# Gated recurrence times a two-layer windowed-attention block: layernorm transposes on half the array's rows, PSUM as one tile of seven banks, and the task order as a table

## The chip, the core and the metric

One NeuronCore of a Trainium2 chip runs the kernel. The metric is the device time in microseconds; the time before is the median of three runs. One more execution was recorded by the hardware profiler, and the profile, its views and its trace all come from that one.

The engines are named as in the profile: PE is the TensorE matmul unit (PEld its weight loads), DVE is VectorE, ACT is ScalarE, POOL is GpSimd, SP is SyncE, which issues the DMAs. PSUM is the memory that PE writes and that DVE and ACT read and write. The kernel uses eight banks of it: seven for its work, each 128 partitions by 512 numbers, and one for a small tile `norms`.

## What is computed

The input `x` is 16 sequences of 512 tokens with 128 channels, in float32. The reference, cut to what matters:

```python
xn = layernorm(x)
# the recurrence
xc = causal_depthwise_conv(xn, conv_w, conv_b)          # 4 taps
r, i = sigmoid(xc @ W_r.T + b_r), sigmoid(xc @ W_i.T + b_i)
a = sigmoid(log_a) ** (8 * r)
h[t] = a[t] * h[t-1] + sqrt(clip(1 - a*a, 0))[t] * (i * xc)[t]
s = rmsnorm(h @ W_out.T) * gamma
# two layers of attention and feed-forward, on xn
for l in range(2):
    hs = shift_token(y)                                  # half the channels one token late
    q, k, v = split(hs @ wqkv)                           # 8 heads of 64
    q, k = rotary_xpos(l2norm(q) * qs, l2norm(k) * ks)
    o = softmax(mask(8 * q @ k.T)) @ v                   # windows of 64 tokens, this and the one before
    y = y + o @ wo
    f = layernorm(shift_token(y)) * lg + lb
    a, g = split(f @ w1 + b1)                            # 341 each
    y = y + (a * gelu(g)) @ w2 + b2
out = x + s * silu(y)
```

## The kernel before

**Tiles.** A sequence (index `s`, 0 to 15) is four token tiles of 128. The recurrence and the feed-forward work on a whole sequence at a time, with channels on the partitions and 512 tokens along the free axis. Attention works on one token tile (`n`, 64 per layer), with tokens on the partitions for the products `q`, `k`, `v`, and on pairs of tiles (`m`, 32 per layer) for the output projection.

**Tasks.** The work is written down as about 6,500 tasks in `all_work`. A task has a name, an item, an engine and the tiles that it opens or touches. The names that the text uses:

- `ld` loads a sequence; `fbn`, `fag`, `fpw`, `fnm` are its layernorm; `ftx` transposes it to channel-major on PE, `xp` and `xs0` copy that out of PSUM on ACT.
- `c0` to `c3` and `cv` are the convolution, `gr`, `gi` the gates' matmuls, `sc` the scan, `yo` the output matmul of the recurrence.
- `Q`, `K`, `V` are the projections on PE. `sqq`, `sqk` square them on ACT, `rq1`, `rq2`, `rk1`, `rk2` are the rotary products on DVE, `addq`, `addk` and `nrm` finish them on POOL, with `red` and ten small steps `n0` to `n9` on DVE for the norms.
- `tr` transposes q and k on PE, into two banks, one for each half of the array's rows; four copies `kc0`, `kc1`, `qc0`, `qc1` on ACT bring them to SBUF. `sim` is the scores on PE (with the mask as a matmul of its own), into two banks.
- `nmA`, `nmB` are the maxima on DVE, `exA`, `exB` the exponentials with their sums on ACT, `rA`, `rB` the reciprocals on DVE, `PA`, `PB` the scaling on POOL. `PT` transposes the weights on PE, into two banks, `pT0` and `pT1` copy them out on ACT, `PV` is the product with the values, `oT` its copy, `wo` the output projection, `y` its addition on DVE.
- Per layer `l` and sequence: `ltx`, `lbn`, `lag`, `lpw`, `lnm`, `lth`, `lhT` are the layernorm, with two transposes on PE (`ltx` to token-major, `lth` back) and the affine copy `lhT`; `lg`, `la`, `lge`, `lhi`, `lyy`, `lr0`, `lr1` are the feed-forward.
- `tf`, `tn`, `z`, `zs`, `zx`, `ot` are the last transpose, the silu, and the output.

**Order.** `schedule` sets the order of the tasks, and with it each engine's own order. It keeps a clock for each engine and picks, among the tasks that can start soon, the one with the smallest key (a due time, corrected by the tables `TAU` and `SHIFT`). It also gives each PSUM tile its bank. The program is then recorded task by task in that order, and the recording layer puts in the semaphores.

**PSUM.** Each of the seven work banks is a pool of its own, and each use of a bank is a tile of its own with its own name (`q`, `sA`, `o`, ...):

```python
banks = [ctx.enter_context(tc.tile_pool(name=f"bank{i}_", bufs=1, space=PSUM)) for i in range(BANKS)]
...
at[key] = banks[bank].tile([P, INNER], F32, name=key[1], tag="bank")
```

**Tile forms of PE.** A matmul can use the array whole, by halves of its rows, by halves of its columns, or by quarters. The planner prefers the form that PE is in. The six transposes of the layernorms and of the end (`ftx`, `0tx`, `0th`, `1tx`, `1th`, `tf`) use it whole, `tr` and `PT` by row halves, `sim` by quarters, `PV` and `wo` by column halves. The helper `matmul` (the projections, gates and feed-forward) takes the whole array where PE stands in that form, and two column halves else.

Of the kernel before, what the change touches and what calls it, by code (L numbers as in the profile page):

```python
# [30 lines left out]
REACH = 30  # L31
OTHER_MODE = 300
TABLE_KEY = {"ea": "TA", "exA": "TE", "exB": "TE", "rt": "TR"}

ROOM = {
    "0mv": 4, "1mv": 4, "fmv": 3, "g": 2, "gelu": 3, "h": 1, "hT": 2, "hid": 3, "kT": 4, "lx": 1, "max": 8,
    "ms": 3, "nx": 2, "oT": 2, "pT": 2, "pr": 3, "qT": 2, "rot": 4, "s": 4, "sq": 2, "sw": 4, "th": 3, "thi": 2,
    "thr": 2, "vl": 4, "vs": 5, "x": 1, "xS": 5, "xc": 2, "xn0": 1, "xn1": 1, "xnf": 1, "xp": 2, "xtok": 2, "y": 3,
}

TAU = {
    "0a": 216, "0ag": 580, "0bn": -24, "0g": -260, "0ge": 4076, "0hT": -537, "0hi": 2408, "0nm": -68, "0pw": -1261,
    "0r0": 990, "0r1": -2182, "0th": 276, "0tx": 33, "0yy": 4216, "1a": 5294, "1ag": 711, "1bn": -852, "1g": 2433,
    "1ge": 377, "1hT": 69, "1hi": 1970, "1nm": 2033, "1pw": -138, "1r0": -467, "1r1": 3335, "1th": 1298,
    "1tx": 1736, "1yy": 5460, "K": -201, "PA": -1630, "PB": -211, "PT": -5584, "PV": 5164, "Q": -112, "TA": -870,
    "TE": -1741, "TR": -256, "V": 1007, "a2": 2422, "addk": 342, "addq": 331, "c0": 2390, "c1": 4732, "c2": -600,
    "c3": -880, "cv": 4159, "ea": 4106, "exA": 6642, "exB": 6438, "fag": 293, "fbn": 1372, "fnm": 6908,
    "fpw": -474, "ftx": 1447, "gelu": -193, "gi": -1858, "gr": -1619, "in": 687, "kc0": 96, "kc1": 219, "kz": -623,
    "ld": 317, "m": -1641, "mp": -882, "ms": 196, "n0": -604, "n1": -429, "n2": -114, "n3": -1713, "n4": 216,
    "n5": 4588, "n6": -2054, "n7": 964, "n8": 241, "n9": -1574, "nmA": -1790, "nmB": 892, "nrm": -1410, "oT": 1064,  # L50
    "ot": -20, "pT0": -35, "pT1": 493, "qc0": -51, "qc1": 577, "rA": 3056, "rB": 2230, "red": 2587, "rk1": 2345,
    "rk2": 414, "rq1": 966, "rq2": -382, "rt": 6134, "s2": -85, "sc": 5466, "si": 123, "sim": -1328, "sqk": 4277,
    "sqq": 2127, "sr": 988, "ss": -495, "tf": 241, "tn": 4128, "tr": 28, "u": 305, "vc": 153, "vd": 10, "vz": 229,
    "wo": 2798, "xld": 4155, "xp": 513, "xs0": 4048, "xs1": -411, "y": 221, "yo": -419, "z": 254, "zs": 8223,
    "zx": 79,
}

SHIFT = {
    "x": (-481, -1082, -101, 4130, 4541, -2524, -596, -258, 3490, -259, 2561, 600, 228, 314, -1342, -1808),
    "g": (27, -265, -606, -62, -144, -220, 324, -273, -28, -213, 296, -716, 121, -138, 542, -30),  # L60
    "a0": (350, -20, 342, 124, 73, 33, 45, -145, 120, 6, 33, 121, 23, 100, 23, -747),
    "f0": (-268, -741, -170, -150, -78, -208, -321, -26, -268, 17, 69, 64, -154, -367, -424, 38),
    "a1": (491, 246, 7, 125, 21, 9, 412, -60, 139, 236, 260, 323, 25, -521, 1127, 175),
    "f1": (-27, -141, -79, 167, 315, -53, -198, 120, 203, 307, 537, 1298, 1006, 4076, 961, 4073),
# [3 lines left out]
ENGINES = ("PE", "ACT", "DVE", "POOL", "SP")  # L68
AFTER = (
    (0, 210, 220, 225, 225), (200, 120, 160, 150, 160), (220, 177, 120, 160, 160), (96, 85, 65, 0, 60), (2400,) * 5,  # L70
)
SWITCH = (110, 115, 100, 97)
WHOLE, ROWS, QUARTERS, COLUMNS, EITHER = range(5)
LOCKED = "sc", "m", "addq", "addk", "nrm", "PA", "PB", "a2", "u", "zs", "zx"
ROUND, SIM_ROUND = 0, 0
GATED, AHEAD = True, 9
PAUSE = 1000, 3500
TOGETHER = 1
RELOAD = 1450
EXP, GELU, ROOT = 1, 2, 4  # L80


class Work:

    def __init__(self):
        self.names, self.tasks, self.known, self.tiles, self.keys, self.touch = {}, [], {}, [], [], []
        self.stage = self.seq = None  # L90

    def tile(self, kind, *item):
        k = (kind, *item)
        if k not in self.known:
            self.known[k] = len(self.tiles)
            self.tiles.append(kind)
            self.keys.append(k)
            self.touch.append([])
        return self.known[k]

    def add(self, name, item, engine, span, base, after=(), opens=(), touches=(), mode=EITHER, table=0, late=None):

        i, e = len(self.tasks), ENGINES.index(engine)
        self.names[name, item] = i
        opens = [self.tile(*t) for t in opens]
        touches = [self.tile(*t) for t in touches]
        lock = name in LOCKED
        for t in {*opens, *touches}:
            self.touch[t].append(i)
        self.tasks.append(dict(  # L110
            name=name, item=item, stage=self.stage, seq=self.seq, engine=e, span=span, key=base, after=[self.names[a] for a in after],
            opens=opens, touches=[*opens, *(t for t in touches if t not in opens)], mode=mode, table=table, lock=lock,
            late=late,
        ))


def all_work(B, NT, lag=2, lead=1, vdve=(), early=EARLY):
    w = Work()
    add = w.add

    def ln(p, s, base, src, after):
        add(p + "bn", s, "DVE", 780, base, after, touches=[src], opens=[(p + "mv", s)])
        add(p + "ag", s, "DVE", 285, base, [(p + "bn", s)], touches=[(p + "mv", s)])
        add(p + "pw", s, "POOL", 1940 if p == "f" else 1330, base, [(p + "ag", s)], touches=[(p + "mv", s)])
        add(p + "nm", s, *(("ACT", 1550) if p == "f" else ("DVE", 1280)), base, [(p + "pw", s)], touches=[src, (p + "mv", s), ("xn" + p, s)], opens=[("xn" + p, s)] if p == "f" else [])

    def gates(s):
        b = s - lead
        w.stage, w.seq = "x", s
        add("ld", s, "SP", 60, b, opens=[("xtok", s)], late=3500)  # L130
        ln("f", s, b, ("xtok", s), [("ld", s)])
        add("ftx", s, "PE", 450, b, [("fnm", s)], mode=WHOLE, opens=[("bank", "fx", s), ("xp", s), ("xS", s)], touches=[("xnf", s)])
        add("xp", s, "ACT", 480, b, [("ftx", s)], touches=[("xp", s), ("bank", "fx", s)])
        add("xs0", s, "ACT", 480, b, [("ftx", s)], touches=[("xS", s), ("bank", "fx", s)])
        add("xs1", s, "POOL", 700, b, [("xp", s), ("xs0", s)], touches=[("xp", s), ("xS", s)])
        w.stage = "g"
        on_pe, C = s < early, ("bank", "cv", s)
        if on_pe:
            add("c0", s, "DVE", 720, b, [("xp", s)], opens=[("xc", s)], touches=[("xp", s)])
            add("cv", s, "PE", 1714, b, [("xp", s)], opens=[C], touches=[("xp", s)])  # L140
            add("c1", s, "DVE", 660, b, [("cv", s)], touches=[("xp", s), C])
            add("c3", s, "DVE", 660, b, [("c0", s), ("c1", s)], touches=[C, ("xc", s)])
        else:
            add("c0", s, "DVE", 720, b, [("xp", s)], opens=[C], touches=[("xp", s)])
            for k in (1, 2, 3):
                add(f"c{k}", s, "DVE", 660, b, [(f"c{k-1}", s)], opens=[("xc", s)] if k == 3 else [], touches=[("xp", s), C])
        for g in "ri":
            add("g" + g, s, "PE", 857, b, [("c3", s)], opens=[("bank", g, s)] + [("thr", s)] * (g == "r"), touches=[("xc", s)])
            add("s" + g, s, "ACT", 600, b, [("g" + g, s)], touches=[("bank", g, s)] + [("thr", s)] * (g == "r"), table=EXP | GELU)
        add("ea", s, "ACT", 720, b, [("sr", s)], touches=[("thr", s)], table=EXP)  # L150
        add("in", s, "DVE", 660, b, [("si", s)], opens=[("thi", s)], touches=[("bank", "i", s), ("xc", s)])
        add("a2", s, "POOL", 1250, b, [("ea", s)], touches=[("thr", s)], opens=[("g", s)])
        add("m", s, "DVE", 320, b, [("a2", s)], touches=[("g", s)])
        add("rt", s, "ACT", 628, b, [("m", s)], touches=[("g", s)], table=ROOT)
        add("u", s, "POOL", 1250, b, [("rt", s), ("in", s)], touches=[("g", s), ("thi", s)])
        add("sc", s, "DVE", 1130, b, [("u", s)], touches=[("thr", s), ("thi", s)], opens=[("h", s)])
# [102 lines left out]
    for s in range(B):  # L259
        gates(s)  # L260
    for l in range(2):
# [4 lines left out]
        for s in range(B):  # L266
            forward(l, s)
# [797 lines left out]
```

## Time and profile before

| | us |
|---|---|
| median of three runs | 1335.42 |
| lowest and highest | 1334.04, 1335.59 |
| the profiled execution, its own time | 1334.82 |
| its span, first to last instruction | 1333.0 |
| PE busy | 1281.7 |
| ACT busy | 1156.0 |
| DVE busy | 1098.5 |
| POOL busy | 1039.9 |

The profile's page has the span, each engine's busy time, then the span in 40 slices with a digit for each engine's busy share and one for the clock that TensorE was granted (9 is full). A group of instructions is given by line, engine, operation and tile, then how often, the busy time, the mean of one in ns, and the idle time before them with what ended it. The table of stretches has, for each stretch of the span, the busy time and number of instructions of each engine, and then the granted clock, the share of the DMA engines and GB/s. A row of the waits has who waited for whom, the time in all, how often, and the longest. A row of the timeline has start and length in us, then the engine, line, operation and tiles. The mean clock over the span is 0.992.

### The profile page before, as it was taken

Reading aid. Unit: us, or ns where it says so; the run is one execution under the profiler, and the core shown is the slowest. Engines: PE = TensorE matmul, PEld = TensorE weight load, DVE = VectorE, ACT = ScalarE, POOL = GpSimd, SP = SyncE. Lnnn points to the kernel's source line nnn. Section 1 sums busy time; section 2 is a strip of 40 time slices with the busy share of each in tenths; the row PEclk is TensorE's granted clock in tenths of the full one; section 3 lists DMA queues with packets and bytes.
Section 4 is the critical chain, followed back from the end, with each engine's and each line's share of the span. In section 5 each row is a group of like instructions: output and inputs, shape, how many; then the busy total and the mean of one; then the engine's idle time right before and its main releaser. Section 6 shows DMA issues by size and latency. Waiting matters only on the chain. (4 is left out here: it accounts for less than half of the span.)

```text
span 1333.0 us, 43632 instructions
## 1 busy us (share of the span) xinstructions
PE 1281.7 (96%) x16988; PEld 729.0 (55%) x16988; DVE 1098.5 (82%) x2752; ACT 1156.0 (87%) x3716; POOL 1039.9 (78%) x1009
## 2 busy tenths in 40 slices
PE   6699999999999999999999999999999999999997
PEld 2355455565555656555564565555646655664563
DVE  7978888988989879788887977989798889848854
ACT  5697989899898989989898988989989979996892
POOL 6896789697887969779696995988778787854862
PEclk9899999999999999999999999999999999999999
DMA  6011011111111111102021111110111011110111
GB/s 207 1 46 33 3 32 33 26 42 33 33 42 38 30 25 38 42 22 65 6 54 25 38 34 33 42 30 22 38 25 46 22 25 38 34 46 21 26 46 40
DMA packets 46766, 49.42 MB, mean 37 GB/s; under 512 B 4704, under 2 KB 31456, under 8 KB 46560
## 3 DMA queue, kind: packets, MB, share of 16 engines
q1 hardware_dynamic: 46560, 46.63, 14.1%
q8 instruction: 135, 2.21, 0.7%
q14 instruction: 71, 0.58, 0.1%
HBM read 13.05 MB, written 4.19 MB: 13 GB/s over the span
## 5 line engine op out<-in xcount | busy, mean ns | idle before, releaser
L722 POOL TENSOR_TENSOR rot<-rot,sw 128x512 f32<-128x512 f32 x256 | 326.2, 1284 | 69.2 <-DVE rot L715 42.0
L846 POOL TENSOR_TENSOR pr<-pr,sum 128x512 f32<-128x512 f32 x256 | 265.1, 1049 | 75.9 <-DVE sum L840 61.0
L759 POOL TENSOR_TENSOR rot<-rot,y 128x1024 f32<-128x1024 f32 x128 | 242.8, 1916 | 37.7 <-DVE y L754 37.3
L832 ACT ACTIVATE pr<-sA,max 128x128 f32<-128x128 f32 x512 | 191.3, 461 | 13.6 <-DVE max L825 7.9
L832 ACT ACTIVATE pr<-sB,max 128x128 f32<-128x128 f32 x512 | 191.3, 458 | 0.6 <-DVE y L754 0.6
L727 DVE TENSOR_REDUCE norms<-sq 128x16 f32<-128x1024 f32 x128 | 155.3, 1213 | 4.9 <-ACT sq L708 2.9
L857 ACT COPY pT<-p 128x512 f32<-128x512 f32 x256 | 151.2, 672 | 5.5 <-PE p L854 4.8
L832 ACT ACTIVATION_READ_ACCUMULATOR pr<-sB,max 128x1 f32 x512 | 145.8, 298 | 0.0
L832 ACT ACTIVATION_READ_ACCUMULATOR pr<-sA,max 128x1 f32 x512 | 145.1, 300 | 0.0
L625 PE MATMUL q<-wqkv,xS 128*64 128x512 f32 (+1 forms) x486 | 136.4, 612 | 4.4 <-ACT pr L832 2.5
L866 PEld LDWEIGHTS o<-pT,vl 128*64 128x64 f32 x2048 | 110.5, 137 | 47.9 <-issue 27.4
L785 ACT COPY qT<-t 128x256 f32<-128x256 f32 x256 | 112.3, 450 | 27.0 <-PE t L780 26.6
L625 PE MATMUL k<-wqkv,xS 128*64 128x512 f32 (+1 forms) x482 | 133.7, 601 | 2.0 <-ACT pr L832 1.6
L625 PE MATMUL v<-wqkv,xS 128*64 128x512 f32 (+1 forms) x464 | 133.5, 604 | 0.9 <-ACT pr L832 0.8
L819 PE MATMUL sA<-kT,qT 64*64 64x128 f32 x2048 | 133.6, 269 | 0.0
L819 PE MATMUL sB<-kT,qT 64*64 64x128 f32 x2048 | 133.2, 269 | 0.0
L866 PE MATMUL o<-pT,vl 128*64 128x64 f32 x2048 | 128.3, 224 | 0.3 <-ACT pT L857 0.3
L866 PE MATMUL o<-pT,vs 128*64 128x64 f32 x2048 | 126.4, 222 | 0.5 <-ACT pT L857 0.4
L819 PEld LDWEIGHTS sA<-kT,qT 64*64 64x64 f32 x2048 | 119.9, 133 | 9.0
L884 PE MATMUL x<-oT,wo 128*64 128x257 f32 x1024 | 123.3, 382 | 0.4 <-ACT pr L832 0.2
L819 PEld LDWEIGHTS sB<-kT,qT 64*64 64x64 f32 x2048 | 119.7, 133 | 0.0
L718 DVE TENSOR_TENSOR sw<-q,table 128x512 f32<-128x512 f32 x128 | 87.4, 683 | 33.7 <-PE q L625 31.0
(154 smaller groups left out, 3206.5 us busy)
## 6 DMA issues: line engine op xcount, KB each, us to landing
vl<-vs SPq DMA_DIRECT2D x224, 128.0 KB, 2.2
xtok<-in_x SPq DMA_DIRECT2D x16, 256.0 KB, 3.1
x<-in_x SPq DMA_DIRECT2D x16, 256.0 KB, 3.1
out<-th SPq DMA_DIRECT2D x16, 256.0 KB, 2.4
wqkv<-in_wqkv SPq DMA_DIRECT2D x2, 768.0 KB, 6.7
w<-in_w SPq DMA_DIRECT2D x2, 384.0 KB, 6.3
rot<-in_rope SPq DMA_DIRECT2D x1, 512.0 KB, 5.6
wo<-in_wo SPq DMA_DIRECT2D x2, 256.0 KB, 5.2
```

Of the source, the lines that this page charges most:

```text
L625: nc.tensor.matmul(ps[col : col + step], w[:, col : col + step], v, start=start, stop=stop)
L718: nc.vector.tensor_tensor(two(at["sw", *n, "qk"[i]]), two(src)[:, :, ::-1, :], two(tab), ALU.mult)
L722: nc.gpsimd.tensor_tensor(r, r, at["sw", *n, "qk"[i]], ALU.add)
L727: nc.vector.tensor_reduce(at["nx", *pair(n)][:, 0, 16 * j : 16 * j + 16], sq, AX.X, ALU.add)
L759: nc.gpsimd.tensor_tensor(flat, flat, bc(at["y", *pair(n)][:, 0, 16 * j : 16 * j + 16], DH), ALU.mult)
L785: nc.scalar.copy(at["qT", *n][:, :, 64 * w : 64 * w + 64], four(at["bank", f"t{w}", *n])[:, 0])
L819: nc.tensor.matmul(out_(w, par)[:, p, :], q[r, p, half[w]], k[r, p, col : col + P], start=False, stop=p == 3)
L832: nc.scalar.activation(at["pr", *n][:, g, :], sim[:, p, :], AF.Exp, bias=at["max", *n, h][:, p : p + 1], accum_out=at["sum", *n][:, g : g ...
L846: nc.gpsimd.tensor_tensor(w, w, bc(at["sum", *n][:, g], P), ALU.mult)
L857: nc.scalar.copy(at["pT", *n][:, w], heads(at["bank", f"p{w}", *n]))
L866: nc.tensor.matmul(o[64 * par : 64 * par + 64, p, 64 * w : 64 * w + 64], at[("vl", "vs")[w], *n][:, h * DH : (h + 1) * DH], pT[:, w, 4 * p ...
L884: nc.tensor.matmul(ps[64 * r : 64 * r + 64, 0 : 2 * P + 1], w, o[:, k, 1 - r : 2 * P + 2 - r], start=k == 0, stop=k == 3)
```

## The change

Three things change together.

1. The six kinds of layernorm and final transposes work on half the array's rows at a time: eight transposes of 64 rows in place of four of 128. The two row halves go to two neighbouring banks (a `pair`), and whoever reads them (`xp`, `xs0`, `lbn`, `lnm`, `lhT`, `tn`, `z`) reads both banks with one access pattern; `z` is two instructions in place of one. `matmul` always uses column halves, so that the form of the whole array is gone.
2. `tr`, `sim` and `PT` also write to a pair of neighbouring banks. The copies `kc0`, `kc1` become one `kc`, `qc0`, `qc1` one `qc`, and `pT0`, `pT1` one `pT`, each over both banks. The seven banks are one PSUM tile, and what a task opens is a slice of it.
3. `all_work` and `schedule` are replaced by `all_tasks`, which only lists the tasks and what they open, and by two tables found by a local search: `PLACES` (each task's place in the order, as steps from one of its kind to the next) and `FIRST_BANK` (the bank, or the first of the two). `in_order` sorts by place.

```diff
-TAU = {
...
-SHIFT = {
...
+PLACES = {
+    "ld": "0 1 7 18 62 120 150 21 1038 175 292 486 483 382 186 598",
+    "fbn": "2 2 12 43 135 36 161 25 1069 128 292 485 485 421 141 605",
...
+FIRST_BANK = {
+    "ftx": "0043025350322002",
...
-def all_work(B, NT, lag=2, lead=1, vdve=(), early=EARLY):
...
-def schedule(w, tau, shift, room):
...
+def all_tasks(B, NT):
...
+                add(n, ("tr", [("pair", "t", *n), ("qT", *n)]), "kc", "qc", ("sim", [("pair", "s", *n), ("pr", *n)]))
...
+def in_order(tasks):
+
+    order, of_name = [], {}
+    for t in tasks:
+        of_name.setdefault(t[0], []).append(t)
+    for name, these in of_name.items():
+        places = np.cumsum([int(v) for v in PLACES[name].split()])
+        for k, (place, t) in enumerate(zip(places, these)):
+            b = int(FIRST_BANK[name][k]) if name in FIRST_BANK and tasks[t] else 0
+            order.append((place, t, b))
+    return sorted(order)
...
-    banks = [ctx.enter_context(tc.tile_pool(name=f"bank{i}_", bufs=1, space=PSUM)) for i in range(BANKS)]
...
+    banks = ctx.enter_context(tc.tile_pool(name="banks", bufs=1, space=PSUM)).tile([P, BANKS, INNER], F32, name="banks")
...
         if kind == "bank":
-            at[key] = banks[bank].tile([P, INNER], F32, name=key[1], tag="bank")
+            at[key] = banks[:, bank, :]
+        elif kind == "pair":
+            at[key] = banks[:, bank : bank + 2, :]
...
+    def halves(ps):
+
+        return ps[:, :, 0 : 64 * NT].rearrange("p r (t k) -> p t r k", k=64)
+
+    def by_halves(v):
+        return v.rearrange("p (t r k) -> p t r k", r=2, k=64)
+
     def transposed(ps, src):
+
         for t in range(NT):
-            nc.tensor.transpose(ps[:, t * P : (t + 1) * P], src[:, t, :], c["ident"])
+            for r in range(2):
+                rows = slice(64 * r, 64 * r + 64)
+                nc.tensor.transpose(ps[:, r, 64 * t : 64 * t + 64], src[rows, t, :], c["ident"][rows, rows])
 
     def token_major(ps, src):
+
         for t in range(NT):
-            nc.tensor.transpose(ps[:, t * P : (t + 1) * P], src[:, t * P : (t + 1) * P], c["ident"])
+            for r in range(2):
+                rows = slice(64 * r, 64 * r + 64)
+                nc.tensor.transpose(
+                    ps[:, r, 64 * t : 64 * t + 64], src[rows, t * P : (t + 1) * P], c["ident"][rows, rows]
+                )
 
     def matmul(ps, w, v, start=True, stop=True):
 
-        step = P if tiling == WHOLE else 64
-        for col in range(0, P, step):
-            nc.tensor.matmul(ps[col : col + step], w[:, col : col + step], v, start=start, stop=stop)
+        for col in range(0, P, 64):
+            nc.tensor.matmul(ps[col : col + 64], w[:, col : col + 64], v, start=start, stop=stop)
...
-    def keep_q(n, w):
-        nc.scalar.copy(at["qT", *n][:, :, 64 * w : 64 * w + 64], four(at["bank", f"t{w}", *n])[:, 0])
...
+    def keep_q(n):
+        nc.scalar.copy(windows(at["qT", *n]), four(at["pair", "t", *n])[:, :, 0])
...
-    def keep_weights(n, w):
-        nc.scalar.copy(at["pT", *n][:, w], heads(at["bank", f"p{w}", *n]))
+    def keep_weights(n):
+        nc.scalar.copy(at["pT", *n].rearrange("p w h d -> p w (h d)"), at["pair", "p", *n])
...
-        th, v = at["th", s], tok(at["bank", "tf", s])
+        th, v = at["th", s].rearrange("p t (r k) -> p t r k", k=64), halves(at["pair", "tf", s])
         if i == 0:
             nc.scalar.activation(th, v, AF.Tanh, scale=0.5)
         else:
-            nc.vector.scalar_tensor_tensor(th, th, 1.0, v, ALU.add, ALU.mult)
+            for r in range(2):
+                part = th[:, :, r, :]
+                nc.vector.scalar_tensor_tensor(part, part, 1.0, v[:, :, r, :], ALU.add, ALU.mult)
...
-    for i, mine, tiling in order:
...
+    for _, t, bank in in_order(tasks):
+        for key in tasks[t]:
+            open_tile(key, bank)
+        do[t[0]](t[1])
+        for f in behind.get(t, ()):
             f()
```

## The prediction

> **What bounds the kernel now.** The page first: the span, the busy shares, the clock row.
>
> ```profile
> span 1333.0 us, 43632 instructions
> PE 1281.7 (96%) x16988; PEld 729.0 (55%) x16988; DVE 1098.5 (82%) x2752; ACT 1156.0 (87%) x3716; POOL 1039.9 (78%) x1009
> ...
> PEclk9899999999999999999999999999999999999999
> ```
>
> TensorE is the bound: 96% busy at almost full clock. But three further engines are busy around 80% at the same time. The busy times of PE, DVE and ACT alone add up to 3,536 us inside 1,333. The kernel lives by their overlap. The waits of TensorE come next, the longest first.
>
> ```profile
> PE fx L615 <- ACT xnf L605: 11.9, 1, 11.9
> PE i L625 <- DVE xc L649: 5.4, 1, 5.4
> PE t L780 <- POOL rot L759: 4.4, 8, 1.0
> PE p L854 <- ACT pr L832: 3.4, 1, 3.4
> ```
>
> These are start-up and single events. In steady state nothing holds TensorE. The table of stretches shows what that looks like in the middle, and what the clock does near gaps:
>
> ```profile
> core 0: us, PE busy (x) PEld busy (x) DVE busy (x) ACT busy (x) POOL busy (x), PEclk, DMA share, GB/s
> 400.00:500.00 100.00, 99.91 (x1348) 56.70 (x1348) 85.17 (x207) 89.60 (x300) 77.69 (x74) 1.00 0.13 31
> ...
> 37.90:41.30 3.40, 1.78 (x2) 0.83 (x3) 3.16 (x13) 0.00 (x0) 0.40 (x1) 0.50 0.00 0
> 41.30:44.70 3.40, 3.40 (x5) 0.96 (x3) 3.40 (x18) 1.35 (x2) 2.70 (x2) 0.50 0.00 0
> 44.70:48.10 3.40, 3.40 (x49) 1.71 (x52) 2.31 (x11) 2.44 (x7) 3.40 (x3) 0.99 0.03 7
> 92.50:95.90 3.40, 2.00 (x40) 1.55 (x32) 2.80 (x4) 3.40 (x8) 3.23 (x5) 1.00 0.02 5
> 95.90:99.40 3.50, 3.05 (x12) 1.26 (x8) 2.92 (x7) 3.50 (x16) 1.82 (x4) 0.51 0.25 75
> 130.10:133.50 3.40, 1.87 (x22) 1.06 (x24) 2.69 (x17) 0.36 (x2) 3.06 (x2) 1.00 0.18 42
> 133.50:136.90 3.40, 3.40 (x20) 1.15 (x18) 2.18 (x6) 1.33 (x6) 3.23 (x4) 0.50 0.00 0
> ```
>
> 100 us of the middle hold 275 us of PE, DVE and ACT work together. And a stretch of 3.4 us in which TensorE was busy 55% or 59% is followed by one at half clock; one at 52% under half clock leaves it there; a full one gives the clock back.
>
> Last, the timeline of the start, where one engine has to wait for the other, for the price of a hand-over.
>
> ```profile
> 11.86 1.63 PE L615 MATMUL fx<-squares,xnf 128*128 128x128 f32 x4 [11.86 <-ACT xnf L605]
> 13.52 0.58 ACT L944 COPY xp<-fx 128x512 f32<-128x512 f32 x1 [0.56 <-PE fx L615]
> 14.01 0.58 ACT L633 COPY xS<-fx 64x512 f32<-64x512 f32 x1
> 14.22 0.92 DVE L647 TENSOR_SCALAR xc<-xp,cols 128x512 f32<-128x512 f32 x1 [4.75 <-ACT xp L944]
> ```
>
> PE ends at 13.49, ACT starts at 13.52; ACT ends at 14.10, DVE starts at 14.22. A hand-over costs 0.03 to 0.12 us after the end, and a copy that is followed by another on its engine costs 0.49 instead of 0.58, because only the last of a run pays its full length.
>
> **The change, part by part.**
>
> *What is meant to be saved.* Per layernorm transpose four 128x128 matmuls become eight on half the rows, two at a time. The rows near it:
>
> ```profile
> L780 PE MATMUL t<-squares,rot 64*128 64x64 f32 x2048 | 89.8, 229 | 5.9 <-POOL rot L759 4.4 <-ACT pT L857 1.0 <-ACT pr L832 0.4
> L619 PE MATMUL 0tx<-squares,xS 128*128 128x128 f32 x64 | 11.1, 289 | 1.3 <-DVE xS L891 1.3
> ```
>
> Start to start in the timeline, sixteen half transposes take 0.50 us, so eight take 0.25; four whole ones take 0.44. 96 such tasks (six per sequence) save 96 x 0.19 = 18 us. Switches between TensorE's tile forms fall from 659 to 621 in the built order; at about 0.1 us (the gap between runs of two forms) 4 us. Joining two copies into one saves ScalarE's fixed part: 450 ns for 256 columns and 672 for 512 give 228 fixed, times 384 joined pairs = 87 us, but of an engine that is not the bound: counted as nothing while TensorE covers it. ACT gets 7 more table loads of 1.28 us, DVE 16 more `z` halves: under 15 us, covered too. With all else equal: about -22 us.
>
> *What else moves.* All seven banks become slices of one tile, `banks`. The built programs can be read without running them, and I read what each instruction waits for. Before, an instruction on PSUM is preceded, in program order, by one on another engine 5,925 times, and waits for that preceding run in 820. After, there are 3,497 such hand-overs, and 3,469 of them wait for the last instruction of the run just before, whatever its bank. A stretch from the middle (lines of the changed kernel, waits in semaphore counts):
>
> ```
> ACT L679 sqq  reads bank 5                      -> ACT 1093
> PE  L754 tr   writes banks 0,1  waits ACT 1093  -> PE 5458
> DVE L689 rk2  reads bank 2      waits PE 5458   -> DVE 1389
> ACT L848 oT   reads bank 6      waits DVE 1389  -> ACT 1094
> PE  L596 Q/K/V writes bank 5    waits ACT 1094  -> PE 5460
> ```
>
> The copy of bank 6 waits for a product from bank 2, which waits for transposes into banks 0 and 1. So the tile is ordered as a whole: all PSUM work of PE, ACT and DVE is one chain in the order of the table. Each engine's queue stands behind its waiting instruction; POOL and the DMA queue, which feed on them, go idle rather than late. The cover under which three engines worked at once is gone.
>
> *The price of the chain*, from the rows of before, start to start within a run (PE 0.86 for a projection, DVE 0.60 and ACT 0.48 for 512 columns, ACT 1.38 for four exponentials with their sums):
> - PE: 384 Q, K, V + 288 feed-forward + 32 gates at 0.86 = 605; 128 scores at 1.11 = 142; 256 flips at 0.50 = 128; 128 `o` at 0.93 = 119; 64 `x` at 1.74 = 111; 96 transposes at 0.25 = 24; `yo`, `cv` 19. Sum 1,147.
> - ACT: 256 exponentials 353; 128 `pT` of 1,024 columns at 0.92 (two rows' slope carried on) 118; 256 `qT`, `kT` 123; 256 `sq` 123; `vs`, `oT` 123; gelu 56; the rest 69. Sum 965.
> - DVE: 512 rotations 309; 256 maxima 154; `hid`, residuals, `xS` 128; `xn`, statistics 66; taps, `s`, `thi`, `th` 70. Sum 727.
> - 3,497 hand-overs: what the last of a run takes beyond its step (PE 0.17, ACT 0.19, DVE 0.08), plus 0.03 to 0.12 to the next engine: about 0.20 each, 700.
> - DVE and ACT have 528 us of work off PSUM (`norms` reduction, the ten small steps, reciprocals, scan; `xnf`, table loads). In front of a queue it can delay the chain: between 0 and 528; a third, 175, since an engine idles most of the time until its turn.
> - before the first matmul 11.9, after the last 7.3: 19.
>
> At full clock 1,147 + 965 + 727 + 700 + 175 + 19 = 3,733 us.
>
> *The clock.* Those 1,285 PE runs have a mean of 0.9 us, then 2.0 us of other engines. With what it drains, PE is busy about 1.06 of 2.9 us, 37%: below the 55 to 59% that cost the clock above. At half clock it is 2.0 of 3.8, 52%: at the share that did not give it back. The Trainium skill ("TensorE: Matmul & The Clock Gate", section "What's actually happening") says in my words that the half rate comes after a wholly idle window of about 3.4 us. No gap here is that long as a rule, so by that page the clock stays and the sum is 3,733; by the rows it is lost most of the time. I take the rows: 85% of PE's work at half clock, + 0.85 x 1,147 = 975. Ends: 0 and 1,147.
>
> A second rule speaks against the chain: "PSUM — Partial Sum Buffer", section "PSUM bank collisions raise a hardware error", asks for semaphores by bank, not for more, and says that engines on different banks run clean side by side; stretch 400 to 500 agrees. By it the waits are needless, and the sum would be -22. But waits that stand in the program are kept, needless or not.
>
> Sum: 3,733 + 975 = 4,708 against the profiled execution's span of 1,333.0 (1334.8 with what lies around it, 0.6 below the median of 1335.42). I say 4,700.
>
> **The rivals.**
> 1. *The chain, but full clock*: 3,733, with hand-overs from 0.14 to 0.26 and the uncovered work from 0 to 528 some 3,350 to 4,300. For it: the stretch 1321 to 1325 (62% busy) kept its clock, so the edge is near 60%, and long feed-forward runs may hold it. Against: 37% is far below.
> 2. *Faster: the waits are there but come late enough to be free.* Place: each hand-over. If the table were laid so that the earlier instruction is done whenever its follower's turn comes, only the 22 us remain, and perhaps 5 of the start: about 1,308. It needs each wait to be shorter than its engine's own backlog; but the backlog of TensorE is 96% and its follower on ACT cannot begin before it, so it decides at once, from the first hundred hand-overs on. It would also hold if the waits that I read were not those that run.
> 3. *Half a chain*: runs within one engine grow, hand-overs overlap more than I think: 2,500 to 3,400.
>
> **How the numbers follow.** Chain with lost clock 0.78 (own range 4,050 to 5,400: uncovered work, hand-overs and clock share at their ends), chain at full clock 0.15, half a chain 0.03, faster 0.04. The predicted time is that of the first. The range, 3,700 to 5,300, takes most of the first and the middle of the second. Slower by over 0.2% (about what a measurement of this kernel can tell from no change) 0.955, faster 0.04, the rest 0.005.
>
> **What would show it.** In the page after: PE, DVE, ACT shares that together come near 100% (PE about 50% with half clock, 37% without), PE waits in the hundreds of us behind ACT and DVE on other tiles, all named `banks`; PEclk mostly 5; POOL near 25%. In the chain of waits PE, ACT and DVE in turn, where now a few engines lead. The transposes' group halved in TensorE time at equal clock. Wrong would be: PE over 90% busy (rival 2), PEclk at 9 (rival 1), or ACT and DVE busy at once with PE in most stretches.

## The result, and the profile after

| | us |
|---|---|
| before, median (lowest to highest) | 1335.08 (1334.04 to 1335.59) |
| after, median (lowest to highest) | 4698.7 (4697.5 to 4702.4) |
| ratio, with its 95% interval | 3.520 (3.514 to 3.526) |

The changed kernel takes three and a half times as long. The page of its profile, the same rows as before:

```profile
span 4700.5 us, 45000 instructions
...
PE 2484.1 (53%) x17688; PEld 1088.7 (23%) x17688; DVE 1168.2 (25%) x2768; ACT 1242.0 (26%) x3339; POOL 1040.9 (22%) x1009
...
PEclk6555555555555555555555555565555555555555
```

DVE, ACT and POOL have about the work that they had: 1,168 against 1,099 us, 1,242 against 1,156, 1,041 against 1,040. PE has twice its busy time, at half its clock. What is gone is the overlap: the shares of PE, DVE and ACT add up to 104% of the span, where they were 265%. The table of stretches has it in the middle of the run (columns as before: PE, PEld, DVE, ACT, POOL, then the clock):

```profile
400.00:500.00 100.00, 50.59 (x328) 20.22 (x328) 26.78 (x56) 28.94 (x88) 20.07 (x19) 0.52 0.01 2
2000.00:2100.00 100.00, 52.17 (x352) 20.84 (x344) 25.16 (x53) 27.98 (x77) 24.42 (x20) 0.55 0.03 7
```

Laid over each other, the records of the three engines say the same. Before, all three were busy at once for 935 of 1,333 us. After, they are for 10 of 4,700; for 4,107 us exactly one of them is busy, for 205 none.

The waits, all engines, longest first, and then those of TensorE alone (who waited for whom: us in all, times, longest):

```profile
POOL pr L820 <- DVE sum L814: 1070.8, 118, 63.5
POOL rot L693 <- DVE rot L686: 514.8, 49, 31.2
...
DVE max L799 <- PE banks L596: 227.7, 73, 6.5
```

```profile
PE banks L596 <- ACT pr L806: 198.9, 72, 7.0
PE banks L596 <- DVE max L799: 119.9, 67, 5.1
PE banks L596 <- DVE rot L686: 103.1, 57, 3.8
```

Before, TensorE's longest wait was 11.9 us, once, at the start. Now the matmuls of one helper (L596: projections, gates, feed-forward) wait for exponentials (`pr`), maxima and rotary products, whose results they don't use. The largest sums are POOL's; it is starved, and nothing waits long for it. The timeline shows how one such wait leads to the next. A projection of the kernel before comes first, for its length, then the changed kernel:

```profile
408.81 1.03 PE L625 MATMUL q<-wqkv,xS 128*64 128x512 f32 x4
```

```profile
2012.71 1.01 ACT L831 COPY pT<-banks 128x1024 f32<-128x1024 f32 x1 [4.09 <-PE banks L840]
2013.78 0.29 PEld L596 LDWEIGHTS banks<-wqkv,xS 128*64 128x64 f32 x4 [1.30 <-ACT pT L831]
2013.78 1.98 PE L596 MATMUL banks<-wqkv,xS 128*64 128x512 f32 x4 [1.11 <-ACT pT L831]
2015.87 0.69 DVE L799 TENSOR_REDUCE max<-banks 128x4 f32<-128x512 f32 x1 [4.04 <-PE banks L596]
...
2016.59 0.59 ACT L848 COPY oT<-banks 128x512 f32<-128x512 f32 x1 [2.87 <-DVE max L799]
...
2017.23 1.97 PE L596 MATMUL banks<-hT,w 128*64 128x512 f32 x4 [1.48 <-ACT oT L848]
```

The copy of the weights, a projection, a maximum of some scores, the copy of an attention output, a feed-forward matmul: five steps on different data. By the order table they use banks 0 and 1, then 2, 4, 5 and 0, and each begins 0.03 to 0.11 us after the one before it ends. A projection takes 1.98 us, where it took 1.03 at full clock (0.86 to the next start and 0.17 beyond). The small steps of the norms (DVE L705 to L723) run in between, since they touch only SBUF and the tile `norms`.

### The profile page after: what moved, and what is told of

Same layout as the page of the kernel before. It is cut to its first block, busy times and chain, and to the rows that moved or that the text cites. A ratio compares the mean times of both kernels' runs of the same rounds, so it can differ in the third digit from the quotient of the medians.

```text
span 4700.5 us, 45000 instructions
## 1 busy us (share of the span) xinstructions
PE 2484.1 (53%) x17688; PEld 1088.7 (23%) x17688; DVE 1168.2 (25%) x2768; ACT 1242.0 (26%) x3339; POOL 1040.9 (22%) x1009
## 5 line engine op out<-in xcount | busy, mean ns | idle before, releaser
L596 PE MATMUL banks<-wqkv,xS 128*64 128x512 f32 x1536 | 740.6, 1064 | 613.2 <-ACT pr L806 94.7
L820 POOL TENSOR_TENSOR pr<-pr,sum 128x512 f32<-128x512 f32 x256 | 264.6, 1041 | 1350.6 <-DVE sum L814 1070.8
L806 ACT ACTIVATE pr<-banks,max 128x128 f32<-128x128 f32 x1024 | 362.6, 367 | 615.7 <-PE banks L596 196.5
L596 PE MATMUL banks<-hT,w 128*64 128x512 f32 x768 | 357.5, 1034 | 275.2 <-ACT gelu L878 38.7
L840 PE MATMUL banks<-pT,vl 128*64 128x64 f32 x2048 | 220.4, 316 | 235.5 <-ACT pr L806 65.7
L596 PEld LDWEIGHTS banks<-wqkv,xS 128*64 128x64 f32 x1536 | 113.4, 202 | 943.4 <-ACT pr L806 129.8
L858 PE MATMUL banks<-oT,wo 128*64 128x257 f32 x1024 | 228.5, 624 | 103.8 <-ACT pr L806 28.7
L596 PE MATMUL banks<-hid,w 128*64 128x512 f32 x384 | 185.4, 1070 | 137.8 <-ACT pr L806 52.6
L793 PE MATMUL banks<-kT,qT 64*64 64x128 f32 x4096 | 243.4, 407 | 0.0
L793 PEld LDWEIGHTS banks<-kT,qT 64*64 64x64 f32 x4096 | 221.6, 217 | 18.0 <-issue 3.0
L840 PE MATMUL banks<-pT,vs 128*64 128x64 f32 x2048 | 213.8, 309 | 0.0
L806 ACT ACTIVATION_READ_ACCUMULATOR pr<-banks,max 128x1 f32 x1024 | 209.2, 204 | 0.0
```

The lines of the kernel that those rows point to most:

```text
L596: nc.tensor.matmul(ps[col : col + 64], w[:, col : col + 64], v, start=start, stop=stop)
L793: nc.tensor.matmul(out_(w, par)[:, p, :], q[r, p, half[w]], k[r, p, col : col + P], start=False, stop=p == 3)
L806: nc.scalar.activation(at["pr", *n][:, g, :], sim[:, p, :], AF.Exp, bias=at["max", *n, h][:, p : p + 1], accum_out=at["sum", *n][:, g : g ...
L820: nc.gpsimd.tensor_tensor(w, w, bc(at["sum", *n][:, g], P), ALU.mult)
L840: nc.tensor.matmul(o[64 * par : 64 * par + 64, p, 64 * w : 64 * w + 64], at[("vl", "vs")[w], *n][:, h * DH : (h + 1) * DH], pT[:, w, 4 * p ...
L858: nc.tensor.matmul(ps[64 * r : 64 * r + 64, 0 : 2 * P + 1], w, o[:, k, 1 - r : 2 * P + 2 - r], start=k == 0, stop=k == 3)
```

## The experiments

The theory: the loss comes from one PSUM tile for seven banks, which puts all work on PSUM in one line; the idle time that follows then costs TensorE its clock. The first rival: the order table (or the new transposes) is at fault. The second, for the clock part: the clock has nothing to do with how long TensorE is busy, or only a wholly idle window loses it.

**One tile alone, in the kernel before.**

```diff
-    banks = [ctx.enter_context(tc.tile_pool(name=f"bank{i}_", bufs=1, space=PSUM)) for i in range(BANKS)]
+    banks = []
+    for i, k in enumerate((7,)):
+        t = ctx.enter_context(tc.tile_pool(name=f"banks{i}_", bufs=1, space=PSUM)).tile([P, k, INNER], F32, name=f"banks{i}_")
+        banks += [t[:, j, :] for j in range(k)]
...
-            at[key] = banks[bank].tile([P, INNER], F32, name=key[1], tag="bank")
+            at[key] = banks[bank]
```

> The kernel before with one thing changed: its seven banks are slices of one PSUM tile; planner, task order, whole transposes and separate copies stay. Built, it has 3,605 hand-overs on PSUM, 3,590 of which wait for the run just before. Chain theory: the same arithmetic as for the changed kernel, with 96 more hand-overs (about 25 us), the 384 copies not joined (87 us) and the transposes not halved (18 us at full clock): about 4,830 us, between 4,500 and 5,100, PE near 50% busy at half clock. Rival, the order table or the half transposes carry the loss: close to 1,335 us.

Measured: 4763.2 us, 3.569 times before (3.562 to 3.575). Its page:

```profile
span 4758.5 us, 43923 instructions
...
PE 2528.7 (53%) x16988; PEld 1138.5 (24%) x16988; DVE 1160.8 (24%) x2752; ACT 1265.2 (27%) x3716; POOL 1046.5 (22%) x1009
...
PEclk6555555555555555555555555555555555555556
```

It is the page of the changed kernel, without its table, its transposes and its joined copies. The tile alone makes the loss. The rest of the change, on top of it, is worth 4,763 - 4,699 = 64 us, all of it together; what each part has of it is not shown.

**Two tiles and four tiles.** The same edit with `(4, 3)` and with `(2, 2, 2, 1)` in place of `(7,)`.

> The kernel before with its banks as two tiles, one of four and one of three banks. Built, 1,883 of 4,533 hand-overs wait for the run just before (7 tiles: 820 of 5,925; one tile: 3,590 of 3,605 and 4,763 us). Chain theory: the loss goes with the waits, (4,763 - 1,335) / (3,590 - 820) = 1.24 us each, so 1,335 + 1,063 x 1.24 = 2,650 us, between 2,000 and 3,300, because two chains can run beside each other. Rival, it is the width of an access or the size of a tile, not the order: below 1,400.

> The same with four tiles, of 2, 2, 2 and 1 banks: 941 of 5,469 hand-overs wait for the run just before. Chain theory: 1,335 + 121 x 1.24 = 1,485 us, between 1,370 and 1,800. Rival as above: below 1,350.

Measured: 2824.0 us (ratio 2.116, 2.112 to 2.120) and 1763.9 us (1.318, 1.312 to 1.324). The pages, two tiles first:

```profile
PE 1844.2 (65%) x16988; PEld 914.6 (32%) x16988; DVE 1140.5 (40%) x2752; ACT 1232.8 (44%) x3716; POOL 1046.6 (37%) x1009
...
PEclk8677778687777787778878788886697686778878
```

```profile
PE 1404.9 (80%) x16988; PEld 754.4 (43%) x16988; DVE 1119.3 (63%) x2752; ACT 1194.6 (68%) x3716; POOL 1044.6 (59%) x1009
...
PEclk9899999999999999989999999999999999999989
```

With 1, 2, 4 and 7 tiles the time is 4,763, 2,824, 1,764 and 1,335 us, and no access has another width. In the built programs the hand-overs that wait for the run just before go the same way: 3,590, 1,883, 941 and 820. So it is the order that a shared tile imposes, and it grows with the number of banks that share. My line through the counted waits was too low: four tiles cost 429 us, not 150. A likely reason, which no run shows: the count leaves out waits on a run a little further back, which can hold TensorE up too.

**Separate tiles again in the changed kernel.** Each use of a bank is its own tile, a pair is two, and what read a pair is two instructions; table and half transposes stay.

```diff
-            at[key] = banks[:, bank, :]
+            at[key] = banks[bank].tile([P, INNER], F32, name=key[1], tag="bank")
...
-            at[key] = banks[:, bank : bank + 2, :]
+            at[key] = [banks[bank + r].tile([P, INNER], F32, name=f"{key[1]}{'AB'[r]}", tag="bank") for r in range(2)]
...
-        nc.scalar.copy(windows(at["qT", *n]), four(at["pair", "t", *n])[:, :, 0])
+        for w in range(2):
+            nc.scalar.copy(windows(at["qT", *n])[:, w], four(at["pair", "t", *n][w])[:, 0])
```

> The changed kernel with one thing undone: each use of a bank is again a tile of its own in a pool per bank, and a pair is two such tiles; what read both banks in one instruction (copies of q, k and weights, x copies, statistics, the affine copy, the tanh) is two instructions. The order table, the banks it gives and the half transposes stay. Built, 773 of 6,291 hand-overs wait for the run just before. Chain theory: the loss is gone; the savings of the prediction (22 us) are there or partly eaten by 128 more DVE statistics and 80 more ACT copies, so 1,300 to 1,345 us, 1,315 the likeliest. Rival, the order table carries the loss: over 1,600 us.

Measured: 1364.5 us, ratio 1.021 (1.020 to 1.023). The loss is gone but for 29 us. The expected saving isn't there either: it missed its range from above.

**The table and the column halves alone.** The same, with the six transposes of each sequence whole, into the first bank of their pair.

> The changed kernel with two things undone: the banks are tiles of their own again (the copies of q, k and weights two instructions each), and the six layernorm and final transposes use the whole array into one bank, so their readers are one instruction each. What stays of the change is the order table, its banks, and column halves in every other matmul. The kernel with half transposes and the same table took 1,364 us, 29 above before. If the table is to blame: at least as long, 1,360 to 1,385 us, since TensorE has about 12 us more to do. If the 256 more DVE and 80 more ACT instructions of the split readers are: 1,335 to 1,350.

Measured: 1352.2 us, ratio 1.013 (1.012 to 1.015): between the two cases. Both pages, half transposes first:

```profile
span 1362.8 us, 45242 instructions
...
PE 1286.6 (94%) x17688; PEld 709.2 (52%) x17688; DVE 1133.0 (83%) x3024; ACT 1186.1 (87%) x3803; POOL 1040.6 (76%) x1009
```

```profile
span 1351.3 us, 44124 instructions
...
PE 1293.5 (96%) x17304; PEld 715.0 (53%) x17304; DVE 1104.1 (82%) x2768; ACT 1173.2 (87%) x3723; POOL 1039.6 (77%) x1009
```

With the table and whole transposes, span minus PE's busy time is 57.8 us (51.3 before), and PE is busy 11.8 us longer than before: the table and the column halves cost 18 us. How these divide between the two is not shown. The half transposes shorten PE by 7 us, but its idle time rises to 76.2 us, and their split readers add 29 us to DVE and 13 to ACT. Two rows of TensorE's waits with half transposes:

```profile
PE 1thA L587 <- DVE xn L571: 2.7, 5, 1.7
PE 0thA L587 <- DVE xn L571: 2.4, 7, 0.8
```

In all, TensorE waits 9.3 us for `xn`, whose instructions were split, against 1.2 us with whole transposes. That is 8 of the 18 us of added idle time. The rest is spread over many small waits, and whether the second bank of each transpose has a part in it is not shown.

**The half transposes alone, in the kernel before**, with two opened banks in the planner's tasks:

```diff
+def both(nm, s):
+    return [("bank", nm + h, s) for h in "AB"]
...
-        add("ftx", s, "PE", 450, b, [("fnm", s)], mode=WHOLE, opens=[("bank", "fx", s), ("xp", s), ("xS", s)], touches=[("xnf", s)])
+        add("ftx", s, "PE", 260, b, [("fnm", s)], mode=ROWS, opens=[*both("fx", s), ("xp", s), ("xS", s)], touches=[("xnf", s)])
```

> The kernel before with one part of the change alone: the six layernorm and final transposes by row halves into two banks, each a tile of its own, their readers two instructions each; planned by the planner of before with their own lengths and form, nothing else changed. From the half transposes measured in the last run (start to next start 0.30 instead of 0.44 us, 96 times) TensorE has 13 us less to do. If the split readers are covered: 1,322 us, between 1,312 and 1,332. If they cost what they cost in the last run, or the plan is upset: 1,340 to 1,370.

Measured: 1410.5 us, ratio 1.057 (1.055 to 1.059), beyond both cases. Its waits of TensorE:

```profile
PE p L879 <- POOL pr L871: 14.7, 14, 3.8
PE fxA L635 <- ACT xnf L613: 11.9, 2, 11.6
PE 0thA L635 <- DVE xn L618: 7.6, 12, 2.1
```

PE's idle time is 108 us. The split `xn` (L618) holds TensorE up here too, but the longest row is the scaled weights `pr`, which this part does not touch: the planned order as a whole came out worse. A likely reason, not shown, is that the planner's keys belong to the old tasks and that a second bank for each transpose leaves fewer banks for the rest. This run says what such a part costs without new keys, not what it could be worth with them.

**Is it the idle time that costs the clock?** First the control: `norms` in SBUF, which frees the eighth bank. Then fillers: matmuls into that bank behind each run of TensorE, which nobody reads.

```diff
-    norms = ctx.enter_context(tc.tile_pool(name="norms", bufs=1, space=PSUM)).tile([P, 2, 2, 32], F32, name="norms")
+    norms = const.tile([P, 2, 2, 32], F32, name="norms")
```

```diff
+        if busy and begun and t[0] not in on_pe and t[0] not in off:
+            matmul(spare, c["ident"], c["wqkv", 0][:, 0:INNER])
```

(`busy`: the last task on PSUM was PE's; `off`: the tasks that don't touch PSUM; `begun`: from the first `tr` on.)

> The changed kernel with the small tile of the norms in SBUF instead of the eighth bank: the control of the next one. Both theories: no change beyond a per cent, 4,650 to 4,740 us, half clock.

> The same with two matmuls of 64 columns by 512 into the eighth bank behind every run of TensorE (1,267 of them; nobody reads or waits for them, 0.86 us at full clock in an idle gap of about 1.7 us). Theory that the clock is lost because TensorE is busy too little: PE is above 65% busy, PEclk is 9 almost throughout, and the time falls by the 1,150 us that the half rate costs, less 100 to 300 us where a filler is still running when its successor could start: 3,550, between 3,400 and 3,900. Rival, the clock has another cause or is not in the chain: PEclk stays at 5 and the time is 4,700 or longer.

Measured: 4695.9 us at a mean clock of 0.533 for the control, and 3815.7 us at 0.935 with the fillers (ratios 3.518, 3.512 to 3.525, and 2.859, 2.854 to 2.864). 1,267 useless matmul pairs make the kernel 880 us faster.

```profile
PE 2748.3 (72%) x22756; PEld 1045.9 (27%) x22756; DVE 1187.3 (31%) x2768; ACT 1242.0 (33%) x3339; POOL 1043.2 (27%) x1009
...
PEclk6999899999998999999999999999899999999999
```

**How much filling does it take?** First one of the two column halves left out:

> The kernel with fillers, with one matmul of 64 columns by 512 (0.43 us at full clock) in place of two behind each run of TensorE. Counted in the traces so far in windows of 3.41 us: a window at full clock in which TensorE was busy under 45% is followed by one at half clock, one over 50% by a full one; out of half clock leads only a window busy over about 80%. With half the filler, TensorE is busy about (1.03 + 0.43) / 2.8 = 52% of the time at full clock, near the edge at which the clock is lost, and about (2.0 + 0.86) / 3.7 = 77% at half clock, just short of the edge at which it comes back. By this rule with two edges the clock is mixed: mean 0.6 to 0.8, and by the line between the two kernels (0.533 and 4,696 us, 0.935 and 3,816 us) 4,100 to 4,550 us. By the rule that only a window without any work loses the clock, the filler that halves the gaps suffices: clock above 0.9 and 3,700 to 3,850 us.

Measured: 3819.6 us (2.865, 2.857 to 2.873), clock 0.934, PE still 72% busy. That is where the rule of the wholly idle window had put it. But the premise was wrong, and so this run tells nothing of the two rules: in the timeline of the kernel with both halves the two halves mostly start within 0.01 us of each other and run side by side, so that leaving one out takes no time away. It does show that half the array keeps the clock as well as the whole one. Then the width of a filler, 256 and 128 in place of 512:

> The kernel with fillers, each filler 256 numbers wide instead of 512: half its time, since the two halves of the columns run beside each other (leaving one of them out left TensorE 72% busy and the clock at 0.934). In the kernel with fillers TensorE's own work is 1,535 of 3,811 us and the fillers add about 1,210; half of that gives about (1,535 + 650) / 3,650 = 60% busy at full clock, above the edge of 45 to 50% at which a window loses it, and about (2,484 + 1,267 x 0.95) / 4,700 = 78% at half clock, just short of the 80% that bring it back. Rule with two edges: clock between 0.7 and 0.93, 3,750 to 4,350 us. Rule that only a window without any work loses the clock: above 0.9, and below 3,800 us, as shorter fillers delay less.

> Each filler 128 wide, a quarter of its time. Rule with two edges: about (1,535 + 400) / 3,650 = 53% busy at full clock, near the edge, and about (2,484 + 1,267 x 0.55) / 4,700 = 68% at half clock, so that a lost clock seldom comes back: clock below 0.7, over 4,300 us. Rule that only a window without any work loses the clock: above 0.9, below 3,750 us.

Measured: 3955.9 us at 0.849 (2.967, 2.959 to 2.976), and 4433.1 us at 0.640 (3.325, 3.315 to 3.336). Both lie in the ranges of the rule with two edges, and far from those of the other. The page with 128:

```profile
span 4425.6 us, 55122 instructions
...
PE 2738.3 (62%) x22756; PEld 1420.1 (32%) x22756; DVE 1185.4 (27%) x2768; ACT 1240.6 (28%) x3339; POOL 1041.2 (24%) x1009
...
PEclk6666576567667666656666576675657656667567
```

and its table of stretches, cut at the marks of 3.41 us at which the records change the clock (first the length, then PE's busy time; the clock is the third figure from the end):

```profile
1226.40:1229.81 3.41, 1.94 (x14) 0.63 (x10) 0.19 (x1) 2.79 (x9) 2.63 (x5) 1.00 0.00 0
1229.81:1233.22 3.41, 1.42 (x10) 0.61 (x12) 1.25 (x2) 0.69 (x1) 0.00 (x0) 1.00 0.00 0
1233.22:1236.64 3.42, 2.39 (x10) 0.78 (x12) 1.29 (x2) 0.00 (x0) 0.00 (x0) 0.50 0.00 0
1236.64:1240.05 3.41, 2.25 (x10) 0.65 (x9) 0.77 (x2) 0.60 (x1) 0.00 (x0) 0.50 0.00 0
...
1263.94:1267.36 3.42, 2.97 (x40) 2.22 (x40) 0.00 (x0) 0.96 (x2) 0.00 (x0) 0.50 0.00 0
1267.36:1270.77 3.41, 1.65 (x40) 1.19 (x39) 1.52 (x4) 0.53 (x2) 0.00 (x0) 1.00 0.02 5
```

A window with 1.94 us of work (57%) keeps the full clock, one with 1.42 (42%) loses it for the next; at half clock 2.39 and 2.25 us (70%, 66%) don't bring it back, 2.97 us (87%) do. Counted over all such windows of seven kernels (the changed one, one tile, two tiles, and the four with fillers):

| PE busy in the window | now full: next half / next full | now half: next half / next full |
|---|---|---|
| under 40% | 641 / 0 | 669 / 0 |
| 40 to 50% | 236 / 270 | 395 / 0 |
| 50 to 60% | 29 / 626 | 1,037 / 0 |
| 60 to 75% | 1 / 837 | 1,076 / 0 |
| 75 to 80% | 0 / 291 | 290 / 21 |
| 80 to 85% | 0 / 244 | 99 / 112 |
| over 85% | 0 / 556 | 43 / 767 |

The clock is lost below 40 to 50% and comes back above about 80%. Between the two, it nearly always stays as it is.

## Why the prediction was right, step by step

**The mechanism.** One chain through all PSUM work, and a clock lost to it: both are shown, each by an experiment that changes nothing else. The 4,700 us met the 4,698.7 us, but not every term was met:

| term | predicted, us | the changed kernel's trace, us |
|---|---|---|
| PE with the ends of its runs (1,147 + 1,285 x 0.17), at full clock | 1,365 | 1,286 (busy time times granted clock) |
| the half clock | 975 | 1,198 (2,484 busy less 1,286) |
| ACT and DVE with their ends (965 + 727 + 306), where PE is idle | 1,998 | 1,927 |
| their work off PSUM that isn't covered | 175 | 85 |
| gaps of the hand-overs, and the ends of the span | 195 | 205 |
| sum | 4,708 | 4,701 |

- *The ends* are the 700 us for 3,497 hand-overs, laid to the engines: 1,285 PE runs at 0.17, some 1,170 of ACT at 0.19 and 1,042 of DVE at 0.08, and the 176 us left over are the gaps. The trace has the same 3,497 hand-overs on `banks`, with a median gap of 0.03 to 0.12 us by kind (ACT to DVE 0.03, PE to ACT 0.05, ACT to PE 0.05, PE to DVE 0.12): as read from the start of the kernel before.
- *The clock* was mis-sized. 85% of PE's work at half clock was said. In the trace it is 92%, counted as work (96% of its busy time), and the price was 223 us higher by the count of the table. It is an upper figure, as it takes every record to double at half clock: that of a projection goes from 1.03 to 1.98 us. The fillers give 880 us as a lower one: they left 17% of the kernel's own PE time at half clock, and take time of their own.
- *The work off PSUM* was half of what I took: the ten small steps hide beside PE and ACT, as at 2,016.48 to 2,019.00 in the timeline.
- These misses went against each other: that the point was met within 2 us is luck.
- *The own range.* "4,050 to 5,400" does not follow from the ends that it names. With nothing uncovered, 0.14 per hand-over and no work at half clock the sum is 3,348, which is the bottom of rival 1; the upper ends give 5,442.

**The rule on the clock.** The prediction set the trace's windows (55 to 59% lost it, 52% did not give it back) against what the Trainium skill says under "What's actually happening" of "TensorE: Matmul & The Clock Gate": half rate after an idle window of about 3.4 us. The prediction took that as a window without any work. The windows were the right guide in kind: of 1,370 windows of the changed kernel 18 had PE busy below 5%, yet 93% of its time is at half clock. Their edge was read too high. Lost is mostly what is under 45%; of the windows of 50 to 60% only 29 of 655 lost it. "37% at full clock, 52% at half" lies below both edges, so the conclusion held.

**The rule on banks.** By "PSUM — Partial Sum Buffer", semaphores by bank would have been enough. The waits of one tile for all are kept by the chip whether they are needed or not: the four numbers of tiles show what each further bank in a tile costs. The kernel before shows engines on different banks side by side: by the names of the tiles, PE, DVE and ACT are all three at work on PSUM for 578 of its 1,333 us.

**The savings.** *Half transposes*: said 18 us. With separate tiles, 96 of them take a median of 0.46 us from first start to last end, 0.66 when whole, and 0.30 against 0.44 us to the next start in the quickest tenth: 13 us of PE. But PE was busy only 7 us less, and the time was 12 us longer, with their readers split. *Tile-form switches*: 620 instead of 658 in the trace, but the time at those changes, from the last start before to the first after, rose from 189 to 206 us, and most of the rise is idle time (11 us at them before, 25 after); the 4 us are not to be seen. *Joined copies*: `pT` takes 1.01 us for both banks; the 87 us were kept out of the sum while TensorE covers ScalarE. In the chain they may be most of the 64 us by which the changed kernel beats the old order on one tile; no run joins them alone. *"Minus 22 us if all else were equal"* fails on the nearest thing to it: 1,364.5 us, 29 above before. So rival 2, faster, would hardly have come even with free waits. What the wide reads of one tile would be worth with free waits is not shown.

**The signs.** PE at 53% (about 50 was said), the three shares at 104%, PEclk at 5, PE's waits all named `banks`, POOL at 22% (near 25 was said): these came. One sign did not: the group of the transposes was to halve in TensorE time at equal clock. With separate tiles it went from 63.0 to 50.7 us, a fifth less. POOL's starved waits, 1,071 us the longest, were foreseen as idleness and nothing waits long for it.

No version here beats the kernel before; the best is its own order with seven tiles.

## What to carry to other kernels

How PSUM is cut into tiles is how its work is ordered: give each bank a tile of its own, or count in the built program what each instruction waits for before a tile is widened for the sake of a wider access. A kernel that lives by overlap pays twice when it is serialised: once for the sum of its engines, and again when TensorE's share falls under the edge that keeps its clock; then useless matmuls in the gaps can be a gain. And an order table is no gain by itself: with separate tiles and whole transposes this one, together with the column halves, is 1.3% slower than the planner's order.

## What I had not expected of the hardware

- The clock has two edges: TensorE keeps full clock in windows of 3.41 us above 40 to 50% busy, and gets it back only above about 80% at half clock. At about 44% busy half of the full-clock windows lose it; at about 82% half of the half-clock windows regain it, and 82% at half clock is 41% of what full clock can do. One edge on the work done per window would explain both, but no run tells that apart.
- Half the array is enough: fillers on 64 columns held the clock as those on 128 did (0.934 and 0.935).
- More fillers, less time: with none, 128, 256 and 512 wide, the time is 4,696, 4,433, 3,956 and 3,816 us, the clock 0.533, 0.640, 0.849 and 0.935.
